# A fused adaptive-layernorm block on one Trainium2 core: the transposed FFN output, a tile's maximum and subtraction, and the score operands of the next batch are put at other places of a hand-written order

## The chip, the core and the metric

The kernel runs on one core of a Trainium2 chip. The metric is the device time of one execution in microseconds (us). The core's engines each work through a queue of their own, in program order: TensorE (PE, with its weight loads PEld), VectorE (DVE), ScalarE (ACT), GpSimd (POOL) and SyncE (SP, which here only issues DMAs). An instruction waits until the semaphores of what it reads, or overwrites, have been set, and everything behind it on its engine waits with it.

## The reference

```python
# x: (8, 1024, 256) f32; W1: (256, 1024); W2: (1024, 256)
mod = (silu(c) @ wmod).reshape(8, 6, 1, 256)
sa, ca, ga, sb, cb, gb = (mod[:, j] for j in range(6))
ga, gb = (sign * max(abs, 0.25) of each)
h = layernorm(x) * (1 + ca) + sa
scores = einsum("nsd,ntd->nst", h * w_lhs, h * w_rhs)      # 1024 x 1024 for each batch
x = x + ga * einsum("nst,ntd->nsd", softmax(scores, axis=2), h)
h = layernorm(x) * (1 + cb) + sb
x = x + gb * (relu(h @ W1 + b1) @ W2 + b2)
```

## The kernel before

There are eight batches b (0 to 7). Each has 1024 rows, cut into eight tiles of 128 rows; a half g has four tiles (512 rows). The main loop runs over b and, inside, over i = 0 to 7; one pass is called a step here. In step i of batch b TensorE makes the scores of the tile two ahead (`direct`, L410), multiplies the weights of tile i with the values (`product`, L493; the tiles 2, 3, 6 and 7 go in pairs, in `pair_begin`, L544, and `pair_end`, L584, with seven block products for eight), and makes a part of the FFN of the batch before: with `fb = b - 1` and `fg = i // TH`, steps 0 to 3 make half 0 of batch b-1, and steps 4 to 7 make its half 1. The FFN's first layer is made in steps 0, 1, 4 and 5, two column groups c in each; its second layer in steps 2, 3, 6 and 7 (`y_first`, `y_second`).

All matmuls are f32. The order of instructions on each engine is that in which the Python calls are made: `pin` makes each instruction depend on the one before it on its engine. So a call moved in the source is an instruction moved in a queue. Tiles are taken from pools with few buffers: the PSUM pool `ps_a` has four and `ps_s` two, the pool `two` has two of the tag "T" (staging of everything that is transposed) and one of "sc" (the scores of a batch), and the next user of a buffer waits for all readers of the last one.

Names that matter below:
- `direct` (L410, its copy to `sc` on ScalarE L417), `row_max` (`m`, DVE L460, 128x1024), `max_turn` (`pm`, a PE transpose of the maximum, L465), `subtract` (`pT`, DVE L472), `exponent` (ACT L481). `weights` is subtract and exponent. `mirror` transposes the upper score blocks to the lower ones: DVE L433 into `Tm`, four DMA writes to DRAM (`D_m`, L304) and one read back (L307), all on SP.
- `pair_products` (L718): `pa` (2 matmuls), the copy `kept` on ScalarE (L737), `pb` (2), `pc` (2); a function `between`, which is `max_turn`, is called in it. `pair_sums` is four DVE adds (L752, L755, L758, L761), `pair_last` one more matmul into `pa`, a DVE add (L769) and a POOL add (L770). `pair_relu` is two ScalarE instructions (L779, L780). `pair_turn` is four POOL adds (L789 to L792).
- `y_second_sums` makes the FFN output `Y` (its scaling on ScalarE, L843). `y_turn` transposes it on DVE (L853) into `T_y`, writes it to DRAM in four DMAs (`D_y`) and reads it back (`Y<-D_y`). With `hurry=False` the read is put off until the next `move` or `y_add`. `y_add` adds these rows to `x` on POOL (L866, two instructions), `y_out` writes them out.
- `prepare_blocks` transposes the normalized x of the next batch (DVE L320 into `T_a`, DMAs `D_a` and `X_a`). From `X_a` the score operands `lT` and `rT` ("sides") are made by `prepare_turn` (lT on DVE, L362; rT on ScalarE, L366) or by `prepare_turn_apart` (ScalarE alone, L340, two instructions for a side).
- `pair_out` ends a pair of tiles on DVE (L599 to L612), `pair_stats` takes their statistics (L239, L240), `product_out` does both for a single tile (L507, L509, L239, L240). `left_sums` (POOL L564 to L567) and `right_sums` (POOL L529) feed `pair_end`.

The last tile of a batch, 7, is handled in step 5 before: the variable `extra` makes its maximum (`row_max`) at the step's start, its `max_turn` in the second `pair_products`, and its subtraction and exponent at the step's end.

Of the kernel before, what the change touches and what calls it, by code (L numbers as in the profile page):

```python
# [24 lines left out]
def adaln_block_kernel(  # L25
# [14 lines left out]
    B, S, D = x.shape  # L40
# [422 lines left out]
    def max_turn(b, i):  # L463
        pm = ps_t.tile([P, HALF], F32, tag="t", name=f"pm_{b}_{i}")
        nc.tensor.transpose(pm[:, :P], max_t.pop((b, i)).to_broadcast([P, P]), ident)  # L465
        pT_t[b, i] = pm
# [250 lines left out]
    def mm(out, lhsT, rhs):  # L717
        nc.tensor.matmul(out, lhsT=lhsT, rhs=rhs, start=True, stop=True)  # L718

    def pair_products(b, g, c, between=None):  # L720

        if c == 0:
            ffn["f"] = two.tile([P, NI, HALF], F32, tag="f", name=f"f_{b}_{g}", bufs=1)
            if b < B - 1:
                ffn["ft"] = two.tile([P, 3, NH, H2], F32, tag="ft", name=f"ft_{b}_{g}", bufs=1)
        hT, hs = ffn["hT", g]
        n = ts(c, P)
        s1, a22 = (w1[:, k, ds((c + NH) * P, P)] for k in range(2))

        pool, tag = (ps_s, "s") if b == B - 1 else (ps_a, "a")  # L730
        pa = ps_a.tile([P, HALF], F32, tag="a", name=f"pa_{b}_{g}_{c}")
        pb = pool.tile([P, HALF], F32, tag=tag, name=f"pb_{b}_{g}_{c}")
        pc = ps_a.tile([P, HALF], F32, tag="a", name=f"pc_{b}_{g}_{c}")
        mm(pa[:, lo], w1[:, 0, n], hT[:, 0, lo])
        mm(pa[:, hi], s1, hs[:, 0])
        kept = work.tile([P, HALF], F32, tag="kept", name=f"kept_{b}_{g}_{c}", bufs=3)
        nc.scalar.copy(kept, pa)  # L737
        if between:
            between()
        mm(pb[:, lo], w1s[:, 0, n], hs[:, 1])  # L740
        mm(pb[:, hi], w1s[:, 1, n], hs[:, 2])
        mm(pc[:, lo], w1[:, 1, n], hT[:, 1, lo])
        mm(pc[:, hi], a22, hT[:, 0, hi])
        pairs[c] = pa, pb, pc, kept
# [100 lines left out]
                scale=gcol[:, 0, h, b : b + 1], bias=gcol[:, 1, h, b : b + 1],  # L845
            )

    def y_turn(b, g):

        Y = ffn["Y"]  # L850
        T = two.tile([P, NV, NT * V], F32, tag="T", name=f"T_y{b}_{g}")
        for h in range(2):
            nc.vector.transpose(  # L853
                T.rearrange("p a (t h u) -> p a t h u", h=2, u=V)[:, :, :, h, :],
                Y[:, h].rearrange("p (t a v) -> p a t v", a=NV, v=V),
            )
        Y = Y.rearrange("p h r -> p (h r)").rearrange("p (b m) -> p b m", b=NV)
        move(Y, T, NT * V, f"y{b}_{g}", hurry=False)
        ffn["rows", b, g] = Y.rearrange("p b (t h u) -> p t h b u", h=2, u=V)

    def y_add(b, g, q):
# [223 lines left out]
    def turns(b, i):  # L1085

        if b == 0 and i == 3:

            Y = two.tile([P, 2, HALF], F32, tag="Y", name="Y_early", bufs=1)
            Y = Y.rearrange("p h r -> p (h r)").rearrange("p (b m) -> p b m", b=NV)  # L1090
            prepare_blocks(1, 0, Y)
        elif b == 0 and i == 4:
            prepare_blocks(1, 1)
        if b > 0 and i == 2:
            ffn_turn(b - 1, 1)
        if 0 < b < B - 1:
            if i == 5:
                prepare_turn(b + 1, 1)
        if i == (7 if b < B - 1 else 6):
            ffn_turn(b, 0)  # L1100

# [35 lines left out]
    def weights(b, i):  # L1137
        subtract(b, i)
        exponent(b, i)
# [3 lines left out]
    for b in range(B):  # L1143
        for i in range(NT):
# [53 lines left out]
            turn_max = (lambda: max_turn(*late)) if late else (lambda: None)  # L1198


            extra = (1, 1) if (b, i) == (1, 0) else ahead if ahead == (b, NT - 1) else None
            if extra:
                row_max(*extra)
            if first:

                ub, ug = (b - 1, 0) if i >= TH else (b - 2, 1)
                back = i % TH == 0 and ub >= 0
                pair_products(fb, fg, c, turn_max)
                if i == 0:
                    ffn_rstd(b - 1, 1)  # L1210
                elif (b, i) == (B - 1, TH):
                    ffn_rstd(b, 0)
                if (b, i) == (1, 0):
                    weights(*late)
                    late = None
                if c > 0:
                    pair_relu(c - 1)
                pair_sums(fb, fg, c)
                if ahead:
                    mirror(*ahead)  # L1220
                pair_last(fb, fg, c)
                if i == 0:
                    right_sums(b, (3,))
                if c > 0:
                    pair_turn(c - 1)
                if i == 4 and b + 1 < B:
                    prepare_blocks(b + 1, 1)
                    xg_times(b + 1, 1)
                if late:
                    subtract(*late)  # L1230
                pair_products(fb, fg, c + 1, (lambda: max_turn(*extra)) if extra else None)
                pair_relu(c)
                sides_too = i == 4 and b + 1 < B
                if sides_too:
                    prepare_turn_apart(b + 1, 0, 1)
                if late:
                    exponent(*late)
                if sides_too:
                    prepare_turn_apart(b + 1, 0, 0)
                middle(b, i)  # L1240
                pair_sums(fb, fg, c + 1)
                pair_last(fb, fg, c + 1)
                if c == 0 and (b, i - 2) in two_t:
                    pair_stats(b, i - 2)
                if ahead and ahead != extra:
                    row_max(*ahead)
                pair_turn(c)
                if back:
                    for q in range(2):
                        y_add(ub, ug, q)  # L1250
                if i == 5:

                    turns(b, i)
                if c > 0:
                    pair_relu(c + 1)
                    pair_turn(c + 1)
            else:
                half = i % TH - 2
                if i == 3 and b + 1 < B:
                    prepare_stats(b + 1, 1)  # L1260
                if half == 0:
                    pair_begin(b, i, turn_max)
                elif not ahead:

                    pair_end(b, i - 1)
                    pair_out(b, i - 1)
                    pair_stats(b, i - 1)
                if half:
                    y_second(fb, fg, turn_max)
                else:  # L1270
                    y_first(fb, fg)
                if ahead:
                    mirror(*ahead)
                if i == 2 and b + 1 < B:
                    prepare_rstd(b + 1, 0)
                elif i == 3 and b + 1 < B:
                    prepare_rstd(b + 1, 1)
                elif i == 6 and b + 1 < B:
                    ffn_rstd(b, 0)
                elif i == NT - 1 and b == B - 1:  # L1280
                    ffn_rstd(b, 1)
                if half == 0:
                    pair_begin_sum(b, i)
                    if i == 2:
                        weights(*late)
                    left_sums(b, i)
                spare()
                early(b, i)
                if late and i != 2:
                    weights(*late)  # L1290
                middle(b, i)
                if i == 2 and b + 1 < B:
                    load_x(b + 1, 1)
                if i == 3 and b + 1 < B:
                    prepare_norm(b + 1, 1)
                    x_plus(b + 1, 1)
                spare()
                if ahead:
                    row_max(*ahead)
                if half:  # L1300
                    y_second_sums(fb)
                else:
                    y_first_sums()
                spare()
            if extra:
                subtract(*extra)
            if i != 5:
                turns(b, i)
            norms(b, i)
            if extra:  # L1310
                exponent(*extra)
            if not first:
                if half and b < B - 1 or i == 3:
                    y_turn(fb, fg)
                for _ in range(4 if half else 1):
                    spare()
            if first:
                product(b, i)
                product_out(b, i)
            elif half and ahead:  # L1320
                pair_end(b, i - 1)
                pair_out(b, i - 1)
                if i == NT - 1:
                    assert not queue
                    right_sums(b + 1, range(3))
                if i == NT - 1 or b == B - 1:
                    pair_stats(b, i - 1)
# [84 lines left out]
```

## Time and profile before

| | |
|---|---|
| device time, median of 3 runs | 775.72 us (775.11 to 776.67) |
| profiled execution: its device time, its span | 775.09 us, 773.3 us |
| PE busy | 760.5 us, 98% of the span, 3708 matmuls |
| PEld busy | 620.6 us, 80% |
| DVE busy | 573.3 us, 74%, 1234 instructions |
| ACT busy | 365.8 us, 47% |
| POOL busy | 541.5 us, 70% |
| granted PE clock | 0.999 |

The span is the time from the first to the last instruction of the program; the device time has 1.8 us more around it. A busy share is an average over eight like batches; one batch takes about 92 us, from the start of the pair product of tile 6 at 516.12 us to the same point of the next batch at 608.46 us. A row of the timeline has start, duration, engine, line, operation and tiles, and in brackets the idle time of the engine before the instruction with what ended it. Matmuls overlap, so their rows are longer than the distance from one to the next: one call of `mm` is two matmul instructions in the trace, and the next one starts 0.43 us later.

### The profile page before, as it was taken

The numbers are of one execution on the slowest core, as the hardware profiler recorded it, in microseconds if no ns is written. First come the engines' busy times: TensorE is split into PE (matmuls) and PEld (weight loads), VectorE is DVE, ScalarE is ACT, GpSimd is POOL, SyncE is SP. The second block draws the span as 40 slices with busy tenths as digits, with TensorE's granted clock in tenths as the row PEclk, the third lists the DMA queues.
The fourth block names the chain that finished last, engine by engine and source line by source line (L and its number), as shares of the span: only waits on it lengthen the run. The fifth ranks groups of instructions, "written<-read, shape, count | busy, mean of one in ns | idle before, by whom it ended". The sixth has DMA issues, their size and how long they took to land.

```text
span 773.3 us, 11483 instructions
## 1 busy us (share of the span) xinstructions
PE 760.5 (98%) x3708; PEld 620.6 (80%) x3708; DVE 573.3 (74%) x1234; ACT 365.8 (47%) x669; POOL 541.5 (70%) x632
## 2 busy tenths in 40 slices
PE   8999999999999999999999999999999999999998
PEld 3576788888887888878887888878888788889886
DVE  6697879768796787957888687876879677694632
ACT  3464546535555355544546344553546535251511
POOL 5543894967959587686868779497794958559641
PEclk9999999999999999999999999999999999999999
DMA  5414334355443464433543554435534345232220
GB/s 193 123 50 146 110 102 130 123 154 169 118 128 106 136 174 117 139 108 122 182 117 114 152 150 128 112 125 174 164 96 130 103 122 171 62 107 77 82 83 27
DMA packets 106212, 95.18 MB, mean 123 GB/s; under 512 B 29701, under 2 KB 98849, under 8 KB 106153
## 3 DMA queue, kind: packets, MB, share of 16 engines
q1 hardware_dynamic: 98408, 85.81, 38.1%
q10 hardware_dynamic: 7744, 8.65, 3.5%
q8 instruction: 29, 0.48, 0.3%
q14 instruction: 31, 0.25, 0.1%
HBM read 50.62 MB, written 43.81 MB: 122 GB/s over the span
## 4 chain that ended last, share of the span: by engine, by line
PE 81%; DVE 11%; DMA 2%; ACT 2%; POOL 2%; issue 2%; SPq 1%; DVEq 0%; POOLq 0%
PE psc L410 14%; PE po L493 12%; PE pa L718 7%; PE pb L718 6%; PE yc L796 6%; PE ya L796 6%; PE yb L796 6%; PE pc L718 5%; PE pr L584 4%; PE py L901 3%; PE pq L584 3%; PE pp L544 3%; PE yd L796 3%; DVE pT L472 1%; DVE m L460 1%
## 5 line engine op out<-in xcount | busy, mean ns | idle before, releaser
L770 POOL TENSOR_TENSOR f<-f,kept 128x512 f32<-128x512 f32 x64 | 81.6, 1275 | 115.2 <-DVE f L769 90.6
L410 PE MATMUL psc<-rT,lT 128*128 128x512 f32 (+3 forms) x384 | 134.6, 486 | 0.0
L493 PE MATMUL po<-xg,pT 128*128 128x257 f32 x576 | 131.6, 380 | 0.0
L493 PEld LDWEIGHTS po<-xg,pT 128*128 128x128 f32 x576 | 108.8, 190 | 16.0 <-issue 1.0
L410 PEld LDWEIGHTS psc<-rT,lT 128*128 128x128 f32 x384 | 67.6, 190 | 38.0 <-issue 26.3
L417 ACT COPY sc<-psc 128x512 f32<-128x512 f32 (+3 forms) x96 | 44.8, 474 | 100.1 <-PE psc L410 100.1
L472 DVE TENSOR_TENSOR pT<-sc,pm 128x1024 f32<-128x1024 f32 x64 | 77.1, 1204 | 6.8 <-PE pm L465 5.8
L481 ACT ACTIVATE pT<-pT 128x1024 f32<-128x1024 f32 x64 | 67.0, 1047 | 26.5 <-DVE pT L472 26.5
L779 ACT ACTIVATE f<-f 128x512 f32<-128x512 f32 x64 | 40.4, 631 | 82.5 <-POOL f L770 82.5
L460 DVE TENSOR_REDUCE m<-sc 128x1 f32<-128x1024 f32 x64 | 77.0, 1204 | 0.0
L737 ACT COPY kept<-pa 128x512 f32<-128x512 f32 x64 | 37.4, 585 | 80.2 <-PE pa L718 80.1
L718 PE MATMUL pb<-hs,w1s 128*128 128x256 f32 x256 | 66.9, 384 | 1.1 <-DVE f L755 1.0
L718 PE MATMUL pc<-hT,w 128*128 128x256 f32 x256 | 66.0, 380 | 0.0
L634 POOL TENSOR_TENSOR x<-x,rows 128x256 f32<-128x256 f32 x64 | 45.3, 740 | 22.3 <-DVE x L509 11.8
L433 DVE STREAM_TRANSPOSE Tm<-sc 128x896 f32<-128x896 f32 (+6 forms) x49 | 34.7, 707 | 27.5 <-ACT sc L417 27.3
L718 PEld LDWEIGHTS pb<-hs,w1s 128*128 128x128 f32 x256 | 45.7, 191 | 10.5 <-DVE f L755 4.1
L718 PEld LDWEIGHTS pc<-hT,w 128*128 128x128 f32 x256 | 48.3, 190 | 7.2 <-ACT kept L737 0.8
L796 PE MATMUL yc<-f,w2s 128*128 128x256 f32 x224 | 52.1, 379 | 0.0
L796 PEld LDWEIGHTS yc<-f,w2s 128*128 128x128 f32 x224 | 41.5, 190 | 10.1 <-issue 2.9
L791 POOL TENSOR_TENSOR ft<-ft,f 128x256 f32<-128x256 f32 x56 | 41.9, 748 | 4.4
L790 POOL TENSOR_TENSOR ft<-ft,f 128x256 f32<-128x256 f32 x56 | 40.8, 729 | 4.4
L706 POOL TENSOR_TENSOR hs<-hT 128x256 f32<-128x256 f32 x16 | 11.6, 728 | 45.1 <-DVE hT L697 45.1
(165 smaller groups left out, 1701.4 us busy)
## 6 DMA issues: line engine op xcount, KB each, us to landing
D_f<-T_f SPq DMA_DIRECT2D x60, 128.0 KB, 2.3
X_f<-D_f SPq DMA_DIRECT2D x15, 512.0 KB, 4.0
D_a<-T_a SPq DMA_DIRECT2D x56, 128.0 KB, 3.4
D_y<-T_y SPq DMA_DIRECT2D x56, 128.0 KB, 2.7
Y<-D_y SPq DMA_DIRECT2D x14, 512.0 KB, 4.4
out_dram<-x SPq DMA_DIRECT2D x14, 512.0 KB, 4.7
X_a<-D_a SPq DMA_DIRECT2D x13, 512.0 KB, 3.4
x<-in_L_attn_x_dram ACTq DMA_DIRECT2D x12, 512.0 KB, 4.0
```

The costliest lines, as they stand in the source:

```text
L410: nc.tensor.matmul(psc[:, : hi - lo], lhsT=lT_t[b, i // TH][:, k, ts(i % TH, P)], rhs=rT_t[b, n][:, k, lo - n * HALF : HALF], start=(k == ...
L417: nc.scalar.copy(score_row(b, i)[:, lo // V : hi // V, :], psc[:, : hi - lo].rearrange("p (n v) -> p n v", v=V),)
L460: nc.vector.tensor_reduce(m, score_row(b, i), AX.XY, ALU.max)
L472: nc.vector.tensor_tensor(pT.rearrange("p j (a v) -> p j a v", v=V), score_columns(b, i), pm[:, :P].rearrange("p (j a v) -> p j a v", j=1, ...
L481: nc.scalar.activation(pT_t[b, i], pT_t[b, i], AF.Exp)
L493: nc.tensor.matmul(po[:, : D + 1], lhsT=pT[:, t, :], rhs=xg_t[b][:, t, 0 : D + 1], start=(t == 0), stop=(t == NT - 1),)
L584: nc.tensor.matmul(out, lhsT=lhs[:, t, :], rhs=rhs[:, t, :], start=(t == 0), stop=(t == TH - 1),)
L634: queue.append(lambda: nc.gpsimd.tensor_tensor(out, in0, row, op))
L718: nc.tensor.matmul(out, lhsT=lhsT, rhs=rhs, start=True, stop=True)
L770: nc.gpsimd.tensor_tensor(f[:, c::NH, hi], f[:, c::NH, hi], kept[:, None, hi].to_broadcast([P, 2, H2]), ALU.add,)
L791: add(ft[:, 2, c], ft[:, 1, c], f[:, c + NH, lo], ALU.subtract)
L796: nc.tensor.matmul(out, lhsT=lhs(c), rhs=rhs(c), start=(c == 0), stop=(c == NH - 1))
```

## The change

It does six things.
1. In `pair_products` the call of `between` (the `max_turn`) stands behind the two `pb` matmuls instead of before them.
2. Tile 7 is no longer `extra`: its maximum is taken at the end of step 5, and its `max_turn`, subtraction and exponent come in step 6, between the two halves of the pair product.
3. The sides of the next batch's second half move from `prepare_turn` at the end of step 5 to `prepare_turn_apart` in the middle of step 5, so that lT too is made on ScalarE.
4. `y_turn` of the first half moves behind `pair_out` (end of step 3); that of the second half stays in step 7 and gets `hurry=True`, and its `y_add` moves to the first part of step 0.
5. In step 0, the relu and `pair_turn` of the second column group move from step 1 to the end of step 0, and the last `right_sums` moves behind the first `pair_turn`.
6. `pair_stats` of the tiles 2 and 3 moves from step 4 to step 6.

```diff
@@ pair_products
         nc.scalar.copy(kept, pa)
+        mm(pb[:, lo], w1s[:, 0, n], hs[:, 1])
+        mm(pb[:, hi], w1s[:, 1, n], hs[:, 2])
         if between:
             between()
-        mm(pb[:, lo], w1s[:, 0, n], hs[:, 1])
-        mm(pb[:, hi], w1s[:, 1, n], hs[:, 2])
@@ y_turn
-    def y_turn(b, g):
+    def y_turn(b, g, hurry=False):
...
-        move(Y, T, NT * V, f"y{b}_{g}", hurry=False)
+        move(Y, T, NT * V, f"y{b}_{g}", hurry)
@@ turns
-        if 0 < b < B - 1:
-            if i == 5:
-                prepare_turn(b + 1, 1)
@@ the main loop
-            extra = (1, 1) if (b, i) == (1, 0) else ahead if ahead == (b, NT - 1) else None
+            extra = (1, 1) if (b, i) == (1, 0) else None
...
-                if c > 0:
+                if i == TH + 1:
                     pair_relu(c - 1)
                 pair_sums(fb, fg, c)
                 if ahead:
                     mirror(*ahead)
                 pair_last(fb, fg, c)
-                if i == 0:
-                    right_sums(b, (3,))
-                if c > 0:
+                if i == 0 and back:
+                    for q in range(2):
+                        y_add(ub, ug, q)
+                if i == TH + 1:
                     pair_turn(c - 1)
...
                 pair_products(fb, fg, c + 1, (lambda: max_turn(*extra)) if extra else None)
+                if i == 5 and b + 1 < B:
+                    prepare_turn_apart(b + 1, 1, 1)
+                    prepare_turn_apart(b + 1, 1, 0)
                 pair_relu(c)
...
-                if c == 0 and (b, i - 2) in two_t:
-                    pair_stats(b, i - 2)
                 if ahead and ahead != extra:
                     row_max(*ahead)
                 pair_turn(c)
-                if back:
+                if i == 0:
+                    right_sums(b, (3,))
+                    pair_relu(c + 1)
+                    pair_turn(c + 1)
+                elif back:
                     for q in range(2):
                         y_add(ub, ug, q)
-                if i == 5:
-                    turns(b, i)
...
                 if half == 0:
-                    pair_begin(b, i, turn_max)
+                    if i == 2:
+                        pair_begin(b, i, turn_max)
+                    else:
+                        pair_begin(b, i, lambda: (max_turn(*late), weights(*late)))
...
+                if i == NT - 2 and (b, 2) in two_t:
+                    pair_stats(b, 2)
...
-                if late and i != 2:
+                if late and half:
                     weights(*late)
...
             if not first:
-                if half and b < B - 1 or i == 3:
-                    y_turn(fb, fg)
+                if i == NT - 1 and b < B - 1:
+                    y_turn(fb, fg, True)
...
                 pair_end(b, i - 1)
                 pair_out(b, i - 1)
+                if i < NT - 1:
+                    y_turn(fb, fg)
```

More of the change, by code (lines that the diff above doesn't have):

```diff
@@ L1306, in adaln_block_kernel @@
                 subtract(*extra)
-            if i != 5:
-                turns(b, i)
+            turns(b, i)
             norms(b, i)
```

## The prediction

> **What bounds the kernel now.** I read the page first: busy shares, slices, and the chain that ended last.
>
> ```profile
> PE 760.5 (98%) x3708; PEld 620.6 (80%) x3708; DVE 573.3 (74%) x1234; ACT 365.8 (47%) x669; POOL 541.5 (70%) x632
> PE   8999999999999999999999999999999999999998
> PEclk9999999999999999999999999999999999999999
> PE 81%; DVE 11%; DMA 2%; ACT 2%; POOL 2%; issue 2%; SPq 1%; DVEq 0%; POOLq 0%
> ```
>
> PE is at work in every slice at its full clock, and the change neither adds nor removes a matmul (tile 7's `pm` only moves). So only PE's gaps can be won or made. The second view is PE's waits (instruction <- releaser: sum, number of times, the mean of one, us):
>
> ```profile
> PE pm L465 <- DVE m L460: 2.7, 6, 0.5
> PE pb L718 <- DVE f L755: 1.0, 2, 0.6
> ```
>
> Idle time understates these gaps, since rows of pipelined matmuls overlap their successors. So I measured on the timeline by how much each matmul starts later than its usual pitch (0.43 us for a call of two). In batches 1 to 6 the excess of steps 4 and 5 is 1.17, 0.76, 1.16, 0.45, 1.52 and 1.17, together 6.2 us. Batch 6 shows the kinds:
>
> ```profile
> 583.22 1.42 DVE L853 STREAM_TRANSPOSE T_y<-Y 128x512 f32<-128x512 f32 x2 [1.06 <-ACT Y L843]
> 586.90 0.34 DVE L612 SCALAR_TENSOR_TENSOR x<-W,rl,x 128x128 f32<-128x128 f32 x1
> 587.75 0.48 DVE L755 SCALAR_TENSOR_TENSOR f<-pb,b_step,u 128x256 f32<-128x256 f32 x1
> 588.28 1.13 PE L718 MATMUL pb<-hs,w1s 128*128 128x256 f32 x4
> 589.40 1.29 DVE L320 STREAM_TRANSPOSE T_a<-xg 128x512 f32<-128x512 f32 x2
> 594.76 1.19 DVE L460 TENSOR_REDUCE m<-sc 128x1 f32<-128x1024 f32 x1
> 596.00 0.32 PE L465 MATMUL pm<-ident,m 128*128 128x128 f32 x1 [0.52 <-DVE m L460]
> ```
>
> The reader is to see DVE running late twice. In step 4 it idles 1.06 us for the last scaling of Y, turns Y, then does `pair_out`; the first `pb` of the next column waits for L755 (0.39 us with its echoes in `pa` and `pc`; absent in batches 2 and 4). In step 5 `pm` starts at 596.00 where the pitch puts it at 595.32: 0.68 us, and 0.10 behind it.
>
> **Part 1: Y's turn behind `pair_out`, `max_turn` behind `pb`.** `pair_out` no longer stands behind the wait for Y. By the rows' own distances its last L612 starts at 585.3 instead of 586.90, the turn runs from 585.6 to 587.0, and L755 ends near 588.0: the step 4 stall goes. `pair_stats` (1.08 us: 593.68 to 594.76) leaves the path of m_6, and `pm` has two `pb` calls more of room. If nothing else moved, all 6.2 us would go.
>
> But tag "T" has two buffers, and T_a takes the one of T_y. T_a can't start before the D_y writes have landed. Batch 2 shows this wait:
>
> ```profile
> 220.39 1.31 DVE L320 STREAM_TRANSPOSE T_a<-xg 128x512 f32<-128x512 f32 x2 [0.42 <-DMA D_y<-T_y]
> 584.67 1.77 SPq L304 DMA_DIRECT2D D_y<-T_y  x4
> 589.20 1.73 SPq L304 DMA_DIRECT2D D_m<-Tm  x4
> 593.52 0.52 SPq L307 DMA_DIRECT2D sc<-D_m  x1
> 599.91 0.34 SPq L307 DMA_DIRECT2D X_a<-D_a  x1
> ```
>
> The last D_y issue there is at 218.00, T_a at 220.39: 2.39 us. With the turn's end 2.35 us later, the four D_y issue at 587.0 to 588.3 and T_a starts at 590.73, not 589.40: 1.33 us later. Queued behind it on DVE are a subtraction, u, L755 to L769 of column 1, and m_6; `pa` and `pb` of column 2 wait for those adds, which meet them just in time (L755 at 594.02, `pa` due at 594.05). m_6 comes 4.28 us after T_a's start (5.36 before, less the statistics' 1.08), ends at 596.2, and `pm`, now due at 595.8, stalls about 0.40. So part 1 wins 6.2 - 6 x 0.40 = 3.8 us. The landing is the uncertain size: 2.03 us (batch 6: last issue 585.99, landed 588.24, less margin) gives a stall near 0.05; the page's D_y median, 2.7, gives 0.75.
>
> **Part 2: sides on ScalarE.** They leave these rows (lT on DVE, rT on ACT):
>
> ```profile
> 603.66 1.70 DVE L362 TENSOR_SCALAR lT<-X_a,sides 128x512 f32<-128x512 f32 x2 [0.27 <-DMA X_a<-D_a]
> 603.94 1.50 ACT L366 ACTIVATE rT<-X_a,sides 128x512 f32<-128x512 f32 x2
> 602.99 1.04 ACT L481 ACTIVATE pT<-pT 128x1024 f32<-128x1024 f32 x1
> 608.46 1.95 PE L544 MATMUL pp<-xg,pT 128*128 128x129 f32 x16
> ```
>
> Four ScalarE instructions of some 0.72 us (1.50 for two) now stand ahead of the relu of column 2 and of exp(6), and ScalarE reaches them near 600.0, before X_a has landed. Everything on ScalarE then waits for a transfer. Behind the landing: 2.9 us of sides, 1.06 of relu, 1.04 of exp: exp(6) ends 5.05 us after X_a lands, and `pp` needs it. X_a lands 6.8, 6.5, 4.7, 6.9, 6.0 and 4.8 us before `pp` in batches 1 to 6; `pp` itself moves up by what part 1 wins. So batches 1, 2, 4, 5 keep 0.4 to 1.2 us of slack, and 3 and 6 would stall 1.0 and 0.8. Those two are late because their D_m writes were slow: in batch 3
>
> ```profile
> 312.55 3.44 SPq L304 DMA_DIRECT2D D_m<-Tm  x4
> q8 instruction: 29, 0.48, 0.3%
> ```
>
> took 3.44 us to issue instead of 1.73, and a 16 KB packet of the instruction queue lies at 313.5 (another at 591.2 in batch 6). [...] by the rows, two of six transfers that this change puts on the path are late, and 1.8 us go. Instruction streams hardly shift, but a fetch can hit another place: bounds 0 and 1.9, I take 1.0.
>
> **Part 3: tile 7 in step 6.** Its subtraction now runs inside the pair product, exp(7) ends about 4.5 us after `pp` starts, and the copies to `sc` of the next batch's tile 0 wait for that subtraction. Cover: the copy, W and Y scaling that `ya`'s second half needs end 4.95 us after `pp`, needed at 5.36; the mirror of tile 0 is about 2.5 us late, its read back lands at +12.7, needed at +13.7. Cost nothing; if 0.4 more were lost there, six batches would lose up to 2.4.
>
> **Part 4: batch 1 and batch 7.** In batch 1, step 0, the subtraction that stands ahead of u waits for a `pm` that comes 0.87 us later: L755 ends 83.35, `pb` due 83.11; with echo -0.4 us (bounds 0 and 0.9). In batch 7 there is no T_a, and the statistics stand before u already, so T_y (1.34 us) is pushed ahead of L755: it ends 681.4, `pb` due 680.34, a new stall of 1.1; its step 5 wins 0.9 of 1.19. Net -0.15. In batch 5, 0.46 us of its stall is a DVE gap with no releaser ahead of L755 that can come back: -0.2 as its expected share.
>
> **Costed at nothing.** POOL's adds of column 1 start 1.2 us later and its last sums end near 618.6, needed at 624.7. In step 0 `y_add` stands before L770 of column 1: it starts at 638.9 behind the Y read (lands near 637) and L770 follows 0.4 late, with `pair_turn` earlier by a step, and no PE wait: next needed is the second layer in step 2. The last right sum is used 15 us later. SP: D_y is issued before D_m as now; with `hurry` the Y read stands in SP's queue until D_y has landed, 632.6, and D_m of tile 2 is issued at 637.2; out goes earlier. X_f's chain runs 1 us late behind PE's `yb`, which gates it anyway. `pm` behind `pb` in steps 0, 1 and 4 has no stall there to lose; each could cost up to 0.4 once if the subtraction that follows delays u, as in batch 1.
>
> **Sum.** 3.8 - 1.0 - 0.4 - 0.15 - 0.2 = 2.1 us. The profiled execution took 775.1 (span 773.3, 1.8 around it) and would take 773.0; the median of the runs is 0.63 higher, so 775.72 - 2.1 = 773.6.
>
> **Rivals.**
> A, the forecast: 773.6, own range 772.4 to 774.8. Chance 0.45.
> B, the new waits stay small: D_y lands in about 2.03 us, X_a is on time: 6.2 - 0.3 - 0.4 - 0.15 - 0.2 = 5.2, so 770.6, with partial forms up to 772. For it: batch 6's landing. Against it: batch 2's and 4's 2.39 measured to the very start of T_a. Chance 0.22.
> C, slower: ScalarE waits for X_a in all six batches. X_a hangs on D_a, that on T_a, now 1.33 us later by the wait for D_y. D_a's issue is now queued on SP behind the Y read at 594.20, which stays, so I left X_a's landing as it was. If it moves to 4.7 us before `pp`'s present place, exp(6) ends 0.35 after it: nothing is won and 2.1 lost, with the 0.55 of part 4: 775.72 + 2.7 = 778.4. It decides from a landing later than about 5.8 us ahead of `pp`. For it: batches 3 and 6 now. Against it: four of six. Chance 0.13.
> D, the change doesn't do what it says: the wait only gets another name. If D_y lands in 2.7 us, the stall at `pm` is 0.75 in each batch, wins are 6.2 - 4.5 = 1.7, and parts 2 and 4 take them back: 775.7. Chance 0.20.
>
> **Numbers.** 0.2% is 1.55 us, about what a measurement of this kernel can tell from no change; faster means below 774.17. A lies below it about 7 times in 10, B always, C gives slower in full, D nearly always the same: faster 0.55, same 0.31, slower 0.14. The range 770.8 to 776.6 takes in A, D and most of B and leaves out C and B's far end.
>
> **What would show it.** Right: T_a idles some 1.4 us <-DMA D_y<-T_y in six batches; `pm` still waits near 0.4 in step 5 and `pb` no longer in step 4 of those; `pb` waits about 1.1 near 680 and 0.3 near 83; L362 and L366 lose six pairs each and L340 gains twelve; ACT idles 2 to 3 us for X_a in step 5, and `pp` waits for L481 in one or two batches. Wrong: `pp` waiting in all batches (C), `pm` at 0.7 (D) or near nothing (B), or a PE wait in steps 6, 7 or 0, where I put none.

## The result, and the profile after

The changed kernel takes 772.01 us (median of 8 runs, 771.62 to 774.46) against 775.62 us before (8 runs, 774.78 to 776.67): a ratio of 0.9958, 95% interval 0.9946 to 0.9971, or 3.6 us less. A second set of runs of the same kernel, on another occasion, gave 772.75 us and 0.9968 (0.9955 to 0.998). The forecast was 773.6 us, faster, in a range of 770.8 to 776.6; both sets lie in it.

The profiled execution is not a typical one of its kernel: it took 774.46 us (span 772.7), 2.4 us more than the median, and only 0.6 us less than the profiled execution of before. It is the slowest of its eight runs; that of the second set, 773.75 us, is the slowest of its five. What it has in excess can be read from it. First two lines of its page, then PE's waits and two waits of other engines (who <- releaser: sum, times, longest one, us; the third number is the longest in the prediction's two rows too, where it is called the mean):

```profile
PE 759.6 (98%) x3708; PEld 621.8 (80%) x3708; DVE 565.1 (73%) x1222; ACT 375.4 (49%) x681; POOL 538.2 (70%) x632
PEclk9999999999999999999999999999999999999999
```

```profile
PE pa L718 <- DVE f L755: 1.9, 2, 1.5
...
PE pm L465 <- DVE m L460: 1.1, 6, 0.2
PE pb L718 <- DVE f L755: 0.8, 1, 0.8
...
PE pp L544 <- ACT pT L481: 0.5, 1, 0.5
```

```profile
ACT rT L340 <- DMA X_a<-D_a: 11.9, 6, 3.9
...
DVE T_a L320 <- DMA D_y<-T_y: 11.6, 6, 3.3
```

`pm` still waits six times, but 1.1 us in place of 2.7. The wait at `pb` is down to one place, batch 7. In their place PE now waits at `pa` for L755 and at `pp` for an exponent, where it did not wait before, and two other engines wait some 12 us each for a transfer, VectorE for D_y and ScalarE for X_a. Batch 6 on the timeline:

```profile
585.05 1.30 DVE L853 STREAM_TRANSPOSE T_y<-Y 128x512 f32<-128x512 f32 x2
...
586.81 0.48 DVE L755 SCALAR_TENSOR_TENSOR f<-pb,b_step,u 128x256 f32<-128x256 f32 x1
...
590.09 1.31 DVE L320 STREAM_TRANSPOSE T_a<-xg 128x512 f32<-128x512 f32 x2 [1.54 <-DMA D_y<-T_y]
...
594.38 1.21 DVE L460 TENSOR_REDUCE m<-sc 128x1 f32<-128x1024 f32 x1
...
595.65 0.32 PE L465 MATMUL pm<-ident,m 128*128 128x128 f32 x1 [0.18 <-DVE m L460]
...
602.70 1.52 ACT L340 ACTIVATE rT<-X_a,sides 128x512 f32<-128x512 f32 x2 [3.89 <-DMA X_a<-D_a]
...
604.13 1.50 ACT L340 ACTIVATE lT<-X_a,sides 128x512 f32<-128x512 f32 x2
...
606.58 1.04 ACT L481 ACTIVATE pT<-pT 128x1024 f32<-128x1024 f32 x1
...
607.67 1.16 PE L544 MATMUL pp<-xg,pT 128*128 128x129 f32 x8 [0.48 <-ACT pT L481]
```

Y's turn no longer waits for Y, and L755 is early. Then T_a waits 1.54 us for D_y, m_6 starts 4.29 us behind T_a, `pm` is held. ScalarE idles 3.89 us for X_a, which lands at 602.7; the two sides, a relu and exp(6) stand behind that, exp(6) ends 4.9 us after the landing, and `pp` waits for it.

The excess of PE's start-to-start distances over the usual pitch, by place, in us (echoes of 0.10 behind a wait counted in):

| place | before | after, first profile | after, second profile |
|---|---|---|---|
| step 5, `pm` (and `pb` behind it), batches 1 to 6 | 4.31 | 2.06 | 2.04 |
| step 4, `pb` for L755, batches 1 to 6 | 1.91 | 0 | 0 |
| step 5, `pa` for L755, batches 3 and 5 | 0 | 2.44 | 2.33 |
| step 6, `pp` for exp(6), batch 6 | 0 | 0.75 | 0.10 |
| batch 1, `pb` at 83 us | 0 | 0.40 | 0.40 |
| batch 7, `pb` near 680 us | 0 | 1.06 | 1.06 |
| batch 7, step 5 | 1.19 | 0.18 | 0.18 |
| sum | 7.41 | 6.89 | 6.11 |

The sums differ by 0.5 and 1.3 us from before; the spans (773.3; 772.7; 771.9) by 0.6 and 1.4. Without the third and fourth row, which are late transfers, the change would bring 7.41 - 3.70 = 3.7 us, and 775.62 - 3.7 = 771.9 is what six of the first eight runs took (771.62 to 772.06). That the typical run has few late transfers is inferred from this; no trace shows such a run, and none of the five runs of the second set (772.34 to 773.75) is as fast.

### The profile page after: what moved, and what is told of

It reads as the page before. It is cut to its first block, busy times and chain, and to the rows that moved or that the text cites. A ratio compares the mean times of both kernels' runs of the same rounds, so it can differ in the third digit from the quotient of the medians.

```text
span 772.7 us, 11479 instructions
## 1 busy us (share of the span) xinstructions
PE 759.6 (98%) x3708; PEld 621.8 (80%) x3708; DVE 565.1 (73%) x1222; ACT 375.4 (49%) x681; POOL 538.2 (70%) x632
## 4 chain that ended last, share of the span: by engine, by line
PE 78%; DVE 10%; POOL 4%; DMA 3%; issue 2%; SPq 1%; ACT 1%; DVEq 0%; POOLq 0%
PE psc L410 14%; PE po L493 12%; PE pa L718 7%; PE yc L796 6%; PE ya L796 6%; PE yb L796 6%; PE pc L718 5%; PE pr L584 5%; PE pb L718 4%; PE pq L584 3%; PE py L901 3%; PE yd L796 3%; PE pp L544 3%; DMA D_y<-T_y 2%; DVE pT L472 1%
## 5 line engine op out<-in xcount | busy, mean ns | idle before, releaser
L770 POOL TENSOR_TENSOR f<-f,kept 128x512 f32<-128x512 f32 x64 | 81.5, 1273 | 116.7 <-DVE f L769 84.6
L718 PEld LDWEIGHTS pb<-hs,w1s 128*128 128x128 f32 x256 | 47.8, 190 | 9.1 <-DVE f L755 2.0
L718 PEld LDWEIGHTS pc<-hT,w 128*128 128x128 f32 x256 | 46.7, 192 | 6.9
L789 POOL TENSOR_TENSOR ft<-f 128x256 f32<-128x256 f32 x56 | 40.9, 731 | 0.0
```

Source lines behind the costliest of these rows:

```text
L770: nc.gpsimd.tensor_tensor(f[:, c::NH, hi], f[:, c::NH, hi], kept[:, None, hi].to_broadcast([P, 2, H2]), ALU.add,)
L789: add(ft[:, 0, c], f[:, c + NH, hi], f[:, c, hi], ALU.subtract)
```

## The experiments

Each was timed in five rounds with the kernel before on the same chip. r1 to r4, r5 to r8, r9 to r11 and r12 are four sets, on three chips; from one set to another the ratio compares better than the median. Medians in us, ratio to the kernel before with its 95% interval:

| run | what it is | median | ratio |
|---|---|---|---|
| r1 | the changed kernel again | 772.75 | 0.9968 (0.9955 to 0.998) |
| r2 | before + item 1 | 776.34 | 1.0011 (1.0004 to 1.0018) |
| r3 | after, half of item 4 undone | 771.51 | 0.9947 (0.9934 to 0.996) |
| r4 | after, T_a freed of D_y | 771.36 | 0.9943 (0.9931 to 0.9956) |
| r5 | after, item 6 undone | 779.36 | 1.0046 (1.0031 to 1.0061) |
| r6 | before + items 1 and 6 | 771.03 | 0.9938 (0.9922 to 0.9954) |
| r7 | r4, lT behind exp(6) | 769.70 | 0.9918 (0.99 to 0.9936) |
| r8 | r7, batches 1 and 7 mended, first try | 771.98 | 0.9948 (0.9932 to 0.9965) |
| r9 | r7, batches 1 and 7 mended, second try | 767.52 | 0.9896 (0.9883 to 0.9909) |
| r10 | r9, D_a ahead of two reads on SP | 767.39 | 0.9892 (0.9878 to 0.9907) |
| r11 | after + 12 small matmuls at the start, to shift PE's instructions | 777.79 | 1.0031 (1.0019 to 1.0042) |
| r12 | after, item 3 undone | 773.67 | 0.9975 (0.9967 to 0.9984) |

**r1: which of the late transfers belong to the kernel.** No edit.

> The changed kernel once more, unchanged. Theory: of the late transfers in its first profile (T_a 3.3 us late in batch 3, pb's release late in batch 5, X_a late in batch 6) most come and go from one execution to the next, so the median stays near 772.0 and a profile of an execution near 772 shows under 1 us of PE excess at pa in step 4 and at pp, while the 0.35 us at pm in step 5 of all six batches, the 0.40 in batch 1 at 83 us and the 1.05 in batch 7 at 681 us stay. Rival: the three stalls belong to the kernel; then they stand in this profile at the same places and sizes (1.8, 0.65, 0.75 us) and its time is near 774.4.

Measured: 772.75 us; the profiled execution took 773.75. Theory and rival each got a part. Batch 6's stall at `pp` fell from 0.75 to 0.10 and batch 5's from 0.65 to 0.36; batch 3's stayed, 1.90 for 1.79, at the same place. VectorE and PE of this second profile:

```profile
309.79 0.48 DVE L755 SCALAR_TENSOR_TENSOR f<-pb,b_step,u 128x256 f32<-128x256 f32 x1
...
314.94 1.30 DVE L320 STREAM_TRANSPOSE T_a<-xg 128x512 f32<-128x512 f32 x2 [3.41 <-DMA D_y<-T_y]
...
317.77 0.48 DVE L755 SCALAR_TENSOR_TENSOR f<-pb,b_step,u 128x256 f32<-128x256 f32 x1
...
318.31 0.70 PE L718 MATMUL pa<-hT,w 128*128 128x256 f32 x2 [1.63 <-DVE f L755]
```

By T_a's start D_y lands some 1.8 us later than in the batches around it (r11 below looks at its packets), and everything queued behind T_a on VectorE, the second L755 included, hands that to PE.

**r2, r6, r5: which edits make the gain.** The forecast put the end of the step 5 stall down to two edits together, without asking what each does alone.

```diff
@@ pair_products, in the kernel before (r2; r6 moves pair_stats(b, 2) to step 6 as well)
-        if between:
-            between()
         mm(pb[:, lo], w1s[:, 0, n], hs[:, 1])
         mm(pb[:, hi], w1s[:, 1, n], hs[:, 2])
+        if between:
+            between()
```

> The kernel before with one edit of the change, the max_turn behind the two pb products. Theory that this edit alone ends the step 5 stall: pm of tile 6 is due 0.87 us later, at about m_6's end, so 0.78 us in four batches, 0.44 and 0.78 in the other two, and 0.28 in batch 7 go, and 0.40 comes in batch 1 at 83 us: about 4.2 less, 771.4 us. Rival, that the gain of the whole change rests on the statistics and the turn of Y moved away from m_6 and from L755: then this alone gives little, 774.5 to 775.6.

Measured: 776.34 us, slower by 0.11%. The theory fell; the rival's range (774.5 to 775.6) missed it too, but its reason was near. PE's waits of r2:

```profile
PE pb L718 <- DVE f L755: 5.1, 7, 1.0
```

The wait at `pm` is gone and stands at `pb` of column 3 instead, at 0.9 to 1.3 us with its echo in five of the batches 1 to 6 (0.44 in batch 4) and 1.3 in batch 7. VectorE in step 5 of batch 6 shows why:

```profile
594.52 0.42 DVE L239 BATCH_NORM_STATS2 st_b<-x 128x6 f32<-128x256 f32 x1
...
595.60 1.19 DVE L460 TENSOR_REDUCE m<-sc 128x1 f32<-128x1024 f32 x1
...
597.97 1.20 DVE L460 TENSOR_REDUCE m<-sc 128x1 f32<-128x1024 f32 x1
599.09 0.48 DVE L752 SCALAR_TENSOR_TENSOR u<-pb,cols,kept 128x256 f32<-128x256 f32 x1
599.60 0.48 DVE L755 SCALAR_TENSOR_TENSOR f<-pb,b_step,u 128x256 f32<-128x256 f32 x1
```

Statistics (1.08 us), m_6, the output of tile 4 and m_7 stand ahead of L755 of column 2, and `pb` of column 3 needs that. Giving `pm` more room only moved the wait.

> The kernel before with two of the change's edits: max_turn behind pb (which alone only turned the wait at pm into one at pb of column 3, for L755 of column 2) and pair_stats of the tiles 2 and 3 in step 6. Theory that these two make the gain: L755 of column 2 comes 1.08 us earlier, which is more than the 0.94 that pb of column 3 waited, so step 5 has no stall over 0.1 although tile 7 is still handled in it; the step 4 stalls of 0.4 in some batches and the 0.40 in batch 1 stay: 771.8 us. Rival, that tile 7's maximum (1.2 us ahead of L755 of column 2) must go too: pb of column 3 keeps waiting 0.5 or more, 774 or above.

Measured: 771.03 us, the theory, and a little better than it. Step 5 of batches 1 to 6 has no excess left. PE's waits have no row for a `pm` behind m any more, and for `pb` only batch 7's (it leaves out the small ones of step 4):

```profile
PE pb L718 <- DVE f L755: 1.0, 1, 1.0
```

The profile keeps 0.39 us in step 4 of each of them, 0.40 in batch 1 at 83 us and 1.31 in batch 7. So items 1 and 6 alone do at least what the whole change does: the median is 1.0 to 1.7 us lower than the changed kernel's two, and the interval (0.9922 to 0.9954) meets that of the first set only at its end (from 0.9946) and that of the second (from 0.9955) not at all. Item 6 without item 1 was not run: m_6 would come 1.08 us earlier in the kernel before, where `pm` waits 0.34 to 0.68 us, so by these rows item 6 might do it alone; that is not shown.

```diff
@@ step 4 and step 6, in the changed kernel (r5)
+                if c == 0 and (b, i - 2) in two_t:
+                    pair_stats(b, i - 2)
                 if ahead and ahead != extra:
                     row_max(*ahead)
...
-                if i == NT - 2 and (b, 2) in two_t:
-                    pair_stats(b, 2)
```

> The changed kernel with pair_stats of the tiles 2 and 3 put back into step 4, ahead of m_6 (all else as changed). Theory that the statistics' 1.08 us in front of m_6 are what the change moved off the path: m_6, and pm in step 5, come 1.08 later, its stall grows from 0.35 to 1.43, six times: 6.5 us more than the changed kernel, 778.5 to 779. Rival, that T_a's wait for D_y or the adds of column 2 set m_6's and pb's time whatever the statistics do: under 2 us more, up to 774.5.

Measured: 779.36 us, the theory (0.4 above its range).

```profile
PE pm L465 <- DVE m L460: 7.4, 6, 1.2
```

The excess at `pm` is 1.36 to 1.41 us in each of six batches. The statistics in front of m_6 are the term that counts, seen from both sides: in r5 they go back in, in r6 against r2 they go out.

**r3, r4: the wait for D_y.** In r3 Y's turn of the first half goes back to its old place, ahead of `pair_out`:

```diff
+                if i == 3:
+                    y_turn(fb, fg)
...
                 pair_out(b, i - 1)
-                if i < NT - 1:
-                    y_turn(fb, fg)
```

> The changed kernel with Y's turn of the first half put back ahead of pair_out, all else as changed. Theory: the move to behind pair_out takes about 1.5 us of stalls at L755 in step 4 away and brings 0.35 x 6 at pm by the wait of T_a for D_y and 1.05 in batch 7, so undoing it wins about 1.7 us: 770.3 us, with pm's wait in step 5 near nothing and pb's wait in step 4 of 0.39 in three or four batches back. Rival, that the move is where the gain comes from: undoing it loses 1 to 3 us, 773 to 775.

Measured: 771.51 us, where r1 took 772.75 in the same runs; the runs themselves (770.03 to 772.56 and 772.34 to 773.75) hardly overlap. The direction is the theory's, the size a little less than its 1.7: the stall at `pb` in step 4 came back in all six batches (0.39 each; before the change it was absent in two), and `pp` of batch 6 waited 1.1 us. The excess at `pm`, at `pa` and near 680 us is gone. Moving the turn behind `pair_out`, the change's first idea, gains nothing in the changed kernel.

```diff
@@ mirror, in the changed kernel (r4)
-        T = two.tile([P, NV, NT * V], F32, tag="T", name=f"Tm_{b}_{i}")
+        T = two.tile([P, NV, V if i == 6 else NT * V], F32, tag="Tm" if i == 6 else "T", name=f"Tm_{b}_{i}", bufs=1 if i == 6 else 2)
```

With Tm of tile 6 in a small buffer of its own, T_a takes the other buffer of the tag "T", and not T_y's.

> The changed kernel with a buffer of its own for the mirror's Tm of tile 6, so that T_a takes another buffer than T_y's and no longer waits for D_y. Theory that the wait for D_y makes the stall at pm: T_a starts about 2 us earlier, right behind L769, pm's 0.35 us goes in all six batches, and so does the late L755 of column 1: 2.1 us less than the changed kernel, 769.9 us. Rival, that m_6 is held by something else (L769 of column 1, which waits for pa): pm's wait stays above 0.2 and the time above 771.5.

Measured: 771.36 us (770.39 to 771.66, all below r1's). T_a follows L769 at once, and the wait at `pm` is gone in every batch, as the theory had it:

```profile
584.02 0.38 DVE L769 TENSOR_TENSOR f<-pa,u 128x256 f32<-128x256 f32 x1
584.33 1.28 DVE L320 STREAM_TRANSPOSE T_a<-xg 128x512 f32<-128x512 f32 x2
```

The sum was not: 1.4 us instead of 2.1. The rest came back at `pp`:

```profile
PE pp L544 <- ACT pT L481: 1.4, 2, 0.9
```

Its excess is 0.76 us in batch 4 and 1.15 in batch 6. PE comes sooner, X_a does not, and the margin ahead of `pp` is used up. One stall's removal is paid for at the next one.

**r12, r7: the sides on ScalarE.** r12 undoes item 3 in the changed kernel:

```diff
-                if i == 5 and b + 1 < B:
-                    prepare_turn_apart(b + 1, 1, 1)
-                    prepare_turn_apart(b + 1, 1, 0)
...
+                if i == 5 and b + 1 < B:
+                    prepare_turn(b + 1, 1)
                 if c > 0:
                     pair_relu(c + 1)
```

> The changed kernel with the sides of the next batch's second half put back to the end of step 5 (lT on VectorE, rT on ScalarE behind the exponent of tile 6), all else as changed. Theory that the sides ahead of exp(6) are a cost of the change and no source of its gain: ScalarE no longer waits for X_a ahead of exp(6), no batch has a stall at pp (0.74 and 0.10 in batch 6 in the two profiles of the changed kernel), and the time is 0.1 to 0.7 us less than the changed kernel's 772.0 to 772.8: 771.3 to 772.3. Rival, that lT on VectorE, waiting for X_a ahead of tile 7's subtraction, is what the change moved off the path: then the stall comes back at pp, ya or psc in step 6 and the time is 773 or above.

Measured: 773.67 us, 0.9 to 1.7 more than the changed kernel in its two sets; the intervals of the ratios overlap, so the time alone does not settle it. `pp` has no wait left, as the theory said, but the rival had the time right: the stall came back in step 6, 0.23 to 0.26 us at `psc` in each of six batches. It is not lT on VectorE, as the rival had thought, but rT on ScalarE, which is now behind relu and exponent, which wait for POOL. The timeline of ScalarE and PE in batch 6:

```profile
601.36 0.63 ACT L779 ACTIVATE f<-f 128x512 f32<-128x512 f32 x1 [3.78 <-POOL f L770]
...
602.36 3.84 PE L410 MATMUL psc<-rT,lT 128*128 128x512 f32 x8
602.42 1.04 ACT L481 ACTIVATE pT<-pT 128x1024 f32<-128x1024 f32 x1
603.37 1.50 ACT L366 ACTIVATE rT<-X_a,sides 128x512 f32<-128x512 f32 x2
```

So item 3 is not the plain cost that was forecast. By these rows rT ahead of the exponent covers a delay that T_a's wait sends through L769, POOL's `y_add` and L770 into ScalarE's queue. In batch 6 of r6, where T_a does not wait, the sides stand at their old place and `psc` has no stall.

r7 is r4 with only lT, which is needed much later than rT, put behind the exponent:

```diff
                     prepare_turn_apart(b + 1, 1, 1)
-                    prepare_turn_apart(b + 1, 1, 0)
                 pair_relu(c)
...
                     exponent(*late)
...
+                if i == 5 and b + 1 < B: prepare_turn_apart(b + 1, 1, 0)
```

> The changed kernel with the buffer of its own for Tm of tile 6 (r4) and, in step 5, lT of the second half made behind the exponent of tile 6 instead of ahead of it. Theory that the sides in ScalarE's queue hold the pair product: exp(6) then ends 3.6 us after X_a lands, not 5.05, and the two stalls at pp in r4's profile (0.76 in batch 4, 1.15 in batch 6) go: 1.0 to 1.9 us less than r4, 769.5 to 770.4 us. Rival, that pp waits for something else behind X_a (tile 6's subtraction, or the new place of lT delays the relu of column 3 and ya): no less than r4, 771.0 to 772.

Measured: 769.70 us, within the theory's range; r7 and r4 are of different sets, and their intervals (0.99 to 0.9936; 0.9931 to 0.9956) meet only at an end. Of the excess at `pp` 0.66 us in batch 6 is left.

**r11: the 16 KB packets as a cause.** The 16 KB packets of q8, the queue that the profile calls instruction, lie close to the late transfers (at 312.48 us in batch 3 of the changed kernel's first profile), so PE's instructions were shifted:

```diff
     warm(D)
+    for _ in range(12): warm(8)
```

> The changed kernel with twelve more warm-up matmuls of 8 columns at the start of PE's program, 48 instructions, so that each 16 KB packet of q8 should come some 5 us earlier against the rest; they cost at most 1 us. Theory that the 1.8 us at pa in batch 3 (T_a 4.2 us after the last D_y issue instead of 2.4, in three of three profiles) come from the packet that starts about 2 us after that issue: the packet lies at 307.8, D_y lands at its usual time and the stall falls below 0.3, batch 6's D_m too is no longer slow; in the profiled execution 1.5 to 2.3 us less, 772 or below. Rival, that batch 3's D_y is late for another reason (its place in DRAM, a load beside it): the stall stays 1.7 to 1.9 with the packet elsewhere.

Measured: 777.79 us (775.87 to 780.12). The price of the edit was misjudged: the twelve matmuls delay the next ones by 4.9 us, and batch 1 at 83 us by 5.8, so packets and work both moved. Relative to the first D_y issue of batch 3 the packet came at -0.09 us instead of 3.1 and 3.5. The stall there fell from 1.8 to 0.47 us, not below the 0.3 of the theory, and it looks different. SP and VectorE of r11, batch 3:

```profile
316.28 2.26 SPq L304 DMA_DIRECT2D D_y<-T_y  x4
320.43 1.31 DVE L320 STREAM_TRANSPOSE T_a<-xg 128x512 f32<-128x512 f32 x2 [1.98 <-DMA D_y<-T_y]
```

The four issues took 2.26 us instead of 1.76, and T_a started 1.89 us behind the end of the four, about as usual (1.96 in batch 6 of the changed kernel's first profile). Batch 6, where the packet now came at -0.07, got a stall at `pa` of 0.84 us that it had not had. T_a started 3.64 to 3.75 us after the first D_y issue in every batch of four profiles (two of the changed kernel, r5, r11) without a packet from 0.2 us before that issue to 3.5 after it, but for two starts at 3.99 and 4.05; with one there it started at 4.15 to 5.59 in six cases, and at 3.72 to 3.75 in three. So the delay mostly goes with the packet, but a packet beside D_y is not enough: with the packet at 3.1 to 3.5 us batch 3 lost 1.8 us and batch 6 nothing, in each of three profiles, and r12's profile has the packet at 312.7 in batch 3 without that stall.

The packets of the kept traces show what differs. One half's D_y is 512 packets of 1 KB. In batch 3 of the changed kernel's first profile the 16 KB packet lies at 312.48 to 313.62 us; 506 of the 512 had started by 312.6, and the last six started from 313.6 on, one after the other until 314.2. From the view of the DMA queues, for 312.65 to 313.55 and for 313.56 to 314.3 us:

```profile
DMA packets 272, 0.03 MB, mean 34 GB/s; under 512 B 272, under 2 KB 272, under 8 KB 272
DMA packets 17, 0.01 MB, mean 10 GB/s; under 512 B 11, under 2 KB 17, under 8 KB 17
```

In the first window no packet has 512 B or more; the second has the six. Batch 3 of r1 and r5 shows the same with two and six packets. In batch 6 of these three and in batch 3 of r12 all 512 had started by 3.2 us after the first issue, and none was held until the end of the 16 KB packet. So the stall of 1.8 us comes where packets of D_y start only behind the 16 KB packet. Why these and no others did is not shown, and the two late starts without a packet stay open.

**r8, r9, r10: a version without the losses.** r8 puts batch 1's `max_turn` back ahead of `pb`, and batch 7's turn of Y into step 4:

```diff
+        if between and (b, g, c) == (0, 0, 0): between()
         mm(pb[:, lo], w1s[:, 0, n], hs[:, 1])
         mm(pb[:, hi], w1s[:, 1, n], hs[:, 2])
-        if between:
+        if between and (b, g, c) != (0, 0, 0):
             between()
...
                 pair_last(fb, fg, c)
+                if (b, i) == (B - 1, TH): y_turn(fb, 0)
...
-                if i < NT - 1:
+                if i < NT - 1 and b < B - 1:
                     y_turn(fb, fg)
```

> As r7 with two more: in batch 1 step 0 the max_turn of column 0 stands before pb as it did, and in batch 7 Y's turn stands behind column 0's sums in step 4 instead of behind pair_out. Theory: the 0.40 us at pb at 83 us and the 1.05 us at pb near 680 us go, nothing comes in their place: 1.4 us less than r7, 768.2 to 769 us. Rival: batch 7's turn only moves its delay to column 1 or to y_add and POOL's adds of column 2 in step 5, and gives under 0.5.

Measured: 771.98 us, 2.3 more than r7: the rival's place (`y_add` and POOL's adds), and worse than it. The excess at 83 and near 680 us is gone. But the timeline of POOL and PE in batch 7 shows a chain (lines behind L735 are one further on in this kernel):

```profile
687.20 2.50 POOL L867 TENSOR_TENSOR x<-x,Y 128x512 f32<-128x512 f32 x2 [2.69 <-DMA Y<-D_y]
689.65 1.26 POOL L771 TENSOR_TENSOR f<-f,kept 128x512 f32<-128x512 f32 x1
...
693.10 1.32 PE L544 MATMUL pp<-xg,pT 128*128 128x129 f32 x8 [2.40 <-ACT pT L481]
```

And its view of windows has a row (from:to, us, busy time of PE, PEld, DVE, ACT and POOL, then the granted clock, DMA share and GB/s):

```profile
694.00:697.40 3.40, 3.40 (x15) 3.16 (x14) 1.22 (x1) 2.25 (x4) 3.24 (x5) 0.50 0.07 9
```

`y_add` waited 2.69 us for the read of Y; the add of column 2 (L770 before, L771 here) stands behind it on POOL, the relu behind that, exp(6) behind the relu. PE idled 2.40 us at `pp`, and from 694.0 its clock was granted at 0.50 for 3.4 us, in which each matmul of the second half of `pp` took 0.10 us longer.

> As r8, but in batch 7 Y's turn stands where it stood before the change, in step 3 ahead of pair_out, as r3 had it there without a stall at 680 us. r8 showed its own place in step 4 to be bad: y_add on POOL waited 2.7 us for the read of Y, the relu and exponent behind it came late, PE idled 2.4 us at pp and its clock was granted at 0.5 for the 3.4 us after. Theory: 0.40 at 83 us and 1.05 near 680 us go against r7, nothing comes in their place, the clock stays full: 768.3 us. Rival: batch 7 keeps a stall in another place, 769.3 or above.

```diff
-                if i == NT - 1 and b < B - 1:
-                    y_turn(fb, fg, True)
+                if (i == NT - 1 and b < B - 1) or (b, i) == (B - 1, 3):
+                    y_turn(fb, fg, i == NT - 1)
```

Measured: 767.52 us (767.32 to 767.61), the theory, and 0.8 better: batch 6's stall at `pp`, at which neither edit aims, was gone in the profile too. Besides 0.09 at `pp` in batch 3 and 0.19 in batch 7's step 5, steps 3 to 6 have no excess.

```diff
@@ move, and mirror's call of it (r10)
         if hurry:
-            read()
+            read_back() if name[0] == "a" and name.endswith("_1") else None; read()
             read_back()
         else:
-            reads.append(read)
+            reads.insert(0, read)
...
-            f"m{b}_{i}",
+            f"m{b}_{i}", i != NT - 2 or b == B - 1,
```

> As r9, and in SP's queue the D_a writes of the second half stand ahead of the two reads (sc of tile 6 and Y), which wait for the landing of D_m and D_y. Theory that X_a is late because D_a waits behind these reads while T_a is long done: D_a is issued near 2 us after T_a's start instead of 5.4, X_a lands 3 to 4 us earlier ahead of pp than in r9, and the last stall at pp (batch 6, 0.56 in r7) goes: 767.5 to 768.0 us. Rival: the landing of D_a itself, or sc's later read, holds pp or tile 6's subtraction: X_a moves by under 1.5 us and the time is not below r9's.

Measured: 767.39 us, and X_a as the theory had it. ScalarE's rT in batch 6, in r9 and then in r10 (`pp` starts at 601.66 and 601.56):

```profile
597.70 1.52 ACT L340 ACTIVATE rT<-X_a,sides 128x512 f32<-128x512 f32 x2 [4.25 <-DMA X_a<-D_a]
```

```profile
593.99 1.52 ACT L340 ACTIVATE rT<-X_a,sides 128x512 f32<-128x512 f32 x2 [0.65 <-DMA X_a<-D_a]
```

Counted from `pp`, rT starts 3.6 us earlier in r10; D_a had stood in SP's queue behind reads that wait for other landings. The time shows little of it, since r9 had almost nothing left to win at `pp`: 0.13 us apart, with overlapping intervals. r10 is 1.1% faster than the kernel before, and it beats the changed kernel by 4.6 to 5.4 us.

## Why the prediction was right, and where its steps were off

*Direction and range were right; the size was 2.1 us forecast, 3.6 measured* (2.9 in the second set). That the number is near is in part luck. The working is one of profiled executions, and these won 0.6 and 1.4 us. Two terms were off in opposite directions: late D_y in batches 3 and 5, put at nothing, cost 2.4 and 2.3 us in the two profiles, and the 1.0 us put down for `pp` cost 0.75 and 0.10.

*Part 1, right in its mechanism and close in size.* T_a took T_y's buffer and waited for D_y; it started 2.34 to 2.44 us after the last issue in most batches (2.39 taken), m_6 came 4.29 behind it (4.28), and `pm` stalled 0.31 to 0.35 us (0.40). 6.22 - 2.06 = 4.2 us won, 3.8 forecast. r4 shows that this wait makes the stall. But two of its reasons do not hold as they stood. The `pb` calls ahead of `pm` win nothing alone (r2), since what stands on VectorE ahead of L755 then holds `pb`; the term that counts is the statistics, 1.08 us (r5, r6). And D_y's landing was bounded by 2.03 and 2.7 us, while T_a in batch 3 started 4.16 and 4.28 us behind the last issue: late landings were reckoned with for D_m and X_a, not for D_y, on which the change had put VectorE's queue.

*Part 2, the term that was mis-sized.* 1.0 us was taken for stalls at `pp`, an estimate between bounds of 0 and 1.9. The chain is as told: exp(6) ended 4.9 us after X_a landed (5.05), in batch 6. It cost 0.75 and 0.10 us in the two profiles, in batch 6 alone. With the bound of 0 the sum would have been 3.1 us, and the typical run is nearer to that than to the 2.1 taken. The profiled executions are nearer to the rows: 2.4 to 3.2 us of late transfers, counting D_y of batches 3 and 5, which the forecast did not have; all but batch 5's 0.36 in the second profile have a 16 KB packet of q8 beside them. That item 3 only costs was wrong: r12 loses 0.23 to 0.26 us per batch without it.

*Part 3, right.* No PE wait in steps 6, 7 and 0 but `pp`'s and batch 1's of part 4.

*Part 4, right.* Batch 1: 0.40 forecast, 0.40 measured. Batch 7: 1.1 and 1.06 near 680 us; its step 5 kept 0.18, where 0.9 of 1.19 was to go. The gap in batch 5's VectorE work, taken at 0.2, did not come back in that form; the batch's 0.65 and 0.36 us come from D_y.

*Rivals.* B (770.6) needed D_y in 2.03 us, but the two times given for it, 585.99 and 588.24, are 2.25 us apart, and where T_a waited it never started sooner than 2.32 us behind the last issue. C did not come: `pp` waited in one batch, not in six. D, the wait with another name, is what happened in single executions: the profiled one won 0.6 us.

## What to carry to other kernels

Take the edits of a reordering apart, and ask of each stall not only what ends it but what is due next on the waiting engine: here a wait at one matmul became one at the next (r2), or at another engine's queue (r4), until the work itself, 1.08 us of statistics, was out of the way. When a transposed or staged tile moves, look whose buffer the next one takes and which landing that waits for; here a buffer of 512 bytes per partition of its own took the new wait away. An instruction that waits for a transfer belongs behind what is due sooner on its queue and does not need it (lT in r7), but not so far that it comes late itself (rT in r12). A DMA issue whose data is ready belongs ahead of those that wait: in r10 this brought X_a 3.6 us forward, though the time, with `pp` no longer waiting, hardly moved.

## What the runs showed of the hardware that was not expected

- The profiles of the kernel before, of the changed kernel and of r10 have 29 packets of 16 KB on q8; in the first two they lie some 26 us apart. With one of them inside, four D_y issues took 4.46 us (r1, at 259.3) and 2.73 us (the changed kernel's first profile, at 259.4), where they took 2.09 us without one in the kernel before (at 259.8). In batch 3 the last two to six of 512 data packets came only behind the 16 KB packet, and T_a started some 1.8 us late; with a 16 KB packet at the same distance and none held (batch 6, and batch 3 of r12), T_a was not late.
- After 2.40 us of PE idle (r8), its clock was granted at 0.50 from 694.0 us on, for 3.4 us, and at 1.00 again from 697.4 to 700. Behind the gap of 1.52 us in batch 3 of the changed kernel's first profile it was granted at 1.00 (318.3 to 321 us).
- The twelve matmuls of 128x128 by 128x8 in r11 delayed what followed by 4.9 us in all, 0.41 us each: two instructions, 0.21 us apart. That is the distance which r8's matmuls of 129 columns had at a granted clock of 0.50, against 0.11 otherwise. At the start of r11 the matmuls of 512 columns follow each other at 0.85 us as late as 13.2 us, where 0.43 is usual, while the changed kernel has 0.43 from 8.1 us on. So behind some 5 us of the small matmuls the distances were still twice the usual ones; why was not tested.
